# Four-layer graph network: layer norm statistics of the last groups, GpSimd waits for VectorE's port, a new written order

## The chip, the cores and the metric

The kernel runs on one core of a Trainium2 chip. The metric is the device time of one launch in microseconds; lower is better. All arithmetic is 32-bit floating point. Engines are named as in the profile: PE is TensorE (matrix products), DVE is VectorE, ACT is ScalarE, POOL is GpSimd and SP is SyncE, which here only issues DMAs.

## The reference

The input x has 128 graphs of 64 nodes with 256 features; adj is a 0/1 matrix of 64 x 64 for each graph. Four layers follow each other, each `x = layernorm(x + layer(x, adj))`:

```python
# layer 0: a GRU over the graph, five steps l
m = h @ weight[l];  agg = A.T @ m;  h = gru_cell(agg, h)      # A = (adj != 0); sigmoid and tanh gates
# layer 1: aggregation and a two-layer MLP (256 -> 1024 -> 256)
out = silu(rmsnorm((adj @ x + epsilon * x) @ W1 + b1)) @ W2 + b2
# layer 2: to the tangent space, aggregate, back to the ball
t = artanh(norm(x)) * x / norm(x);  s = adj @ t;  out = project(tanh(norm(s)) * s / norm(s))
# layer 3: attention with masked softmax
h = x @ W.T + b;  u = adj * exp(e[:, None] + f[None, :] + ab);  out = (u / sum(u)) @ h
```

What matters here is the layer norm at the end of each layer: mean and variance of each row of 256 features, then `(x - m) / sqrt(v + 1e-5)`.

## The kernel before

Two graphs are packed into a block of 128 rows; four blocks make a group, and there are 16 groups (g = 0 to 15, `NG` = 16). A group goes through all four layers in SBUF. The five GRU steps take by far the most TensorE time. Products by blocks (`gate`, `prod`, `by_sums`, `by_sums_back`) use seven products where plain block multiplication has eight, at the price of sums on VectorE.

The last group, 15, is cut into two pieces of two blocks after its MLP (layer 1), each a stream of its own, so that their short dependent steps overlap. They get `y1` and `adjT` from the group.

**Order.** `Flow` collects every instruction as an operation with an engine (or a choice of two), an assumed cost `us`, the buffers read and written, and for some the mark `port`. The string `ORDER`, made beforehand outside this file, says in which order the operations of up to six streams are issued, and on which engine. `issue` emits them and ties each to the one before it on its engine, so the order within an engine is fixed; between engines only data dependencies make waits. The assumed costs and the `kb` of DMAs have no other use in the file.

**Port.** Marked `port` are the GpSimd operations made by `pool` (sums `pool_sum`, powers, small ones `few` and `few_s`), and VectorE's elementwise work with all its operands in SBUF: `summing`, the updates of hT, `times_state`, `scaled` and `tan`.

**Statistics of a layer norm** (`layer_norm`). For groups 0 to 13 (`summed = g < NG - 2`):

- `onto_rows` (L811) writes y = product * scale + x and gives the sum of each row as a side output (`accum_out`) into `st`; for the second layer norm an extra ScalarE pass (L828) makes that sum.
- GpSimd makes the negative mean `mv`, ScalarE the sum of squared differences by a `Square` pass with side output (L833), GpSimd `ve`, the power `rstd` (L845) and the offset `off`.
- rows are scaled by ScalarE or VectorE.

For groups 14 and 15, VectorE makes the statistics with `bn_stats` (L841) and `bn_aggr` (L842) for each block, and `ve` (L843) and the offset (L854) as well; only the power stays on GpSimd. These two groups also run the small operations of layer 2 (norms, series, `onto_ball`) on VectorE, and the sums of squares `sqt` and `x3 + wb_r` by `summing` on VectorE, where the other groups use GpSimd's `pool_sum` (L448).

Other names below: `hr` (L790) is the DMA that turns hidden state into rows for the next aggregation, `x3T` likewise for attention; `ps_agg` is an aggregation, `p_ga` to `p_gc`, `p_hx`, `p_ix` GRU products, `ps_hr` (L782) the turn of the last hidden state into rows, `p_ah` to `p_ch` the first MLP product (L1109), `p_ox`, `p_oy` the second (L1184), `ps_o` the same for group 15 by plain products, `ps_sup` layer 2's aggregation, `ps_a`, `ps_att` attention; `w2f` sums (L681) prepare weights.

Of the kernel before, what the change touches and what calls it, by code (L numbers as in the profile page):

```python
# [53 lines left out]
class Flow:  # L54

    ENGINES, AHEAD = ("PE", "DVE", "ACT", "POOL", "SP"), 6
    SIGNS = "ABCDEFGHIJKLMNOPQRSTUVWXYZabcdefghijklmnopqrstuvwxyz0123456789!#$%&()*+,-./:;<=>"
    ORDER = ("CEEg~PhD~BNhED~BOiDC~Bs$CAAAAAAAAAAAAAAAAii~Nr~Nr~BO~N.~CU8~B+88~Bt~Bt8$~Bt~BL~Bt88li~BL~FU~FU~FU~FU"
             "~BL!i~Et~BL~Bt!~FZ~Bs~BL~FZ~BpEe~Bt~D%~BL~EO~BLA~DAi~DAB~DA~BoB~Bo~CUBF~BogiFFF~B+~B+HG~B+~GiAA~BK8~"
             "GjEC%~DB%B~BO%~FZAB~C3~BL~Es~E:~B<EA%B~CUlB~Et~BsB~CZBE~C5AB~CaE~BV~B+~C0~DiF,FA~D$H$~CBA~DE~CW~BsA~"  # L60
             "EQA$~BM~EQC&Ag~Dx~DBC~CV~DK~GK~Bs~CVgF&&~DxC~DGF%H~BsfBEF9(~EdA~B:AEj(jBB~Dx~D8~D8~MDAA~CJjkEBjFk~Mh"
             "x(~DA~Np~DAAx~MD~MDGl~BKT~NL~CJAH~DB~BdEA>CBAxe~Bdh~MBC~Lze~BpC~B+~Br!~BNxTA8TCG8~CB~CB~BN8B~J9!9DAD"
             "eAgDACCFB~CXCAAhBh~D8AKA~DABKK~DKKL~By~Do~BNLhFF~BV~BV#K~CAH#~G#PKhP~DA~Ce~B0~DA~Bt~DBKD~CAK~B0~BtPM"
             "~CAA~BV~By~IVA,P+CB8uh~BKA8A~Bp~Bq+gAC~BN~BNF;~BN~FZ~BNFBFBFuD~D%HFD~BQFKDGK~DjM~DF~Bu~BtL~Bt~Bt&M~B"
             "tMFHpFHFk%Fko&ooGoFqFGlopA(GpAlpH~BQA~BygG~CyoC&Ao&CoC~BQhAqGAG8Ag~BrBKGDKMA*DKgnKCh~DFnMDAPJBAKRDfK"
             "BD+B+B+~Bt~BQ~BQ~BQB+~JjEE~EP~D%E~BvpE~I3BK~BQB~BoA~DA~BqAA~BKA~B+~BoC~BM9~CUAA~BV~BVAAACBBC~Bo~Bo~B"
             "Veee!AC9FC~GAf~GAB8~CVABeGAg~EoC~Eo~BL~Bo(~BpA(AAAAB~CyAAKBKKAL!~BtA!kAA~BtCFCFBFFBFHFfHGKAAB~FeBKgK"
             "&CKkGKBMKKBKLBKK-~CA~CAKLM~ByM~ByMK~BU-KM~Bz~ByLK~BU~BVLKpKMKFBMFBKKBKMBKKBKK~BLEKE~BL~Ce~BL~Ce~Eo~C"
             "eEGEGLlL~DA~DA,,FKGKHKL~Bo~BoA~BqAAAG-~BoGC~BoK-9AG~BMAAGCAGAAB!88GC8ACBeeBgAfAC8B8B8BAGAGAC~Eo~BQJC"
             "*~EonA~BQ~BLAJA~BQAABAAAABAA~BMA!AfCACFF9FFBFHeBFfAFBFAgFBHFCKFBFBKqKGMFBHF~B:~B:H,~DALHo~B:L~B:~B:G"  # L70
             "F~BRp~CaKH~B;KFpH~BPBFBM~Bt~BtB%%LFBMBjlj~Bol~Buij~BLij~BL~BP~BLijEG%GL%jj~D8L~BQ~Cy~Bo&~DAFL~BR~H+L"
             "~BRF~H+L~BqF~BLHAALAA~B+~CBC~Bo~BqL~BMA~CUALAC~BVOA~BVAOB8ABsCeOB8CeGAgAfCB~GAF~GA8BA~CVAB~E+CA~BpjC"
             "kAA88AAABA~HUjBF~Bo!9A!AAlAHFGgeCGKKBKKKBMKfAGABFBg+G~CACK~BWBooBKBKM~Ce~BLoKB-~By~Byp~By~B0L~By~CeB"
             "q~CeMKB~HUMBKK~BziFE~BzFp~BUE~BL~BUE~EoL-oGop~Boq~CAp~CA~BL~CyGK~BLlK~BzM~Bo~BLFKG~DeHK~BLAAG~DAAG~B"
             "-A8CG~BoKG~BM8GAAG8CeAGfeBeeeeBg~BuACAgf8C8B~GAB~GAB8~B,AGAA~BQnC~Eo~BQJC~EoLAJ~BLAJ~BpAAABAAAABAA!A"
             "!FeCFFFCFHBF%BFfAABFBEgFGFCjBj(FB~B:~B:~B:BF~BtB(~Bt~Bt~BvGBjHAKHABAAoo~BpKBKLAAAAKG~BW~B:FBMB~BtBM~"
             "G%H~Bu~G%MFDG~BP~BMLF!~BQKgKGkHFCF~CaGFH~EtLDDHKLF~BQKDLCFK9gLFLCFqFDGFKFLFMFGAAFL~BRAACL(FALAALA8CL"
             "AeBA~D8BC8L8f~DAgpAA~CULCF~BVs~DKlAOBHA~BVsFG~BoOABAk~DKGABj~BV~By!kFg~ByFGDl~DKG~BV~DKAH~BVB~DK~DK~"
             "B0KGKK~B0KGC~By~CekM~ByC~CA,D+,~ByC~By~BU~B0B+~BWG~BV&KKMD~By~By~By~By~BWL8KqMAAGKGpCpAKCAAGK~BQAM*B"
             "LAJ~E:BK~BQKgAJ~BQJABCD~Bt~Bt~D%DC~CZ~IZDC~IZ~BQK~BQFFDFFK~CZH%~BvLFAAAAFBDFHFFGAA(AA~C3BH~BP~BPH~BP"  # L80
             "B~BPFlfKKB%~G%Gg+9j!B+KCBoHo~F*~FJ~E7~E7B!KK&gFLA!AA&ACAGKGCFApA-KGA~Bp-AjpqjBMAAlKBAF~Bu~EtLH~BtpA~"
             "Bt~BLoL~BtpFBKF~BL%LFfq~B:kKFL~BtfMA~D8~D8G~D8AAL(AAAL(AAApAFLAF,AAA9AAfFFL~ByfAHLAHAL~B+~B+~B+~B+~B"
             "Q~BY~B+A~BV~BysA~BKGs~CejkO~D+~BVA&AA~BVAAf~I8G~CefFB~BMF!~IeGGl~DKA~BVAH~FAK~BV~Ey~Ey~BQ~EyK~C!AGK~"
             "CeGK~CC~ByMkAAAG~BWAKG~JK~BU~CfK~CfKK,M~HyGo~BzoL-oKGqKMLnK~BQAnKMB~BdKLgK~BdKM~BQTK~BQCKT~BVKDLx!K>"
             "K!~CenCK~BzxCKLDKJDKD-T~BtK-~EPqKhhM~Bt~ErphoL~CZD~CZLh!~DFDpgDK~BQ~E:~BQFFgLKC~BaDFD~GjqDLF;DM~DjDD"
             "~B:D~FZHL~Bt~Bv~C3L~C3~BRF~Ca~E$~Bt~BP~E$~CaF~E$~CaCFDGDF~B:&DDCjGgjLgjAC~BQjLe~BRLeA~BML%g%Gg~CBjC~"
             "EPp~BRDFFL(FsDDFks~FA~BV~EyslF~BVHO~CZCG%~B:D&FDD&DF~BPGFDDF&(BF(~By9j~E$fH~ByBHKK~B0G~FAKKDG~EU~BM~"
             "Ce~BVFk!~D+~BVM~D++GC+C~CAl~C9F~C9KJ~BUGDK~C9HK~C9K~BWG~IeMDDKp~IALoLqoGM~BU~BUCGoCpogoGKqGGKMKCKKMB"
             "~Bt~BtoBKD~BVEKLEK~BuKEELFFFFFFKk~BWKKG-KGKMGKMIlp~E3(,P~C%LHoLp~C%PHKLPKII~CUqLPO~CUM~BoI~BRuAL~BKl"
             "eHL~CjpeHA!LFFCfIFFgfgeCe9CA~B,HABBBFRF999FF~BLBFHfjFB~E:H>~E:DgGKTKKFG!T%CGL%TFCFLl~D%D~BzH~D%D%~C5"  # L90
             "G%DFB!FkCKPGCKPPPlEGAAgF~CUBMD~CUFC~EUFGAAGCDGKCKIBMAA~BU+pC(H-AfADB~C8~C8KApoppAgDgDpKC~ByLH~DK~DK~"
             "CBCDKM~IACLK+L+DHMKL~GoKAAA,,A+pB+-ID~CfKLKM~By~ByLIAAAA~B,9IKKlBHH+HKK~CefFBFF9IBFHFFFF~CAFFH~BMBH!"
             "FGFG~D%G~D%%~BV%GCFF~Bqk~CZCL~CZ!%G%CBKFFkCKKGKf(~BtBl~BV~Bt~BuKFIMFMLoHAAMf9AAAAHALeHeeILA~BtHpK~BL"
             "MKGIAALLFFqfAAMAAf%HALAAALFFLAALeA~FALAA9AALA~DKfA~DKp~ByLeAAAf/A~DoG/~Bo~BoGs~Bo~BoFBO(AA~BVl888~BV"
             "AAIABFB~IeH~ByIHAAA~BzA~BMAIA~Bz!AABKHxK~EU~BVK~B7CKI~Do~Bd~DoLC~Do~By~B7~CgKD,T~BMK~C9K!>o~C9MTK~Cf"
             "FCTpFFLFoGKpMI~HyMCLoKpFF~CfhMFFkKDD&KlKKMDKD!KM~Ey#kklK~EyG~BUKKHDDhDK~C1DG~CBHKKkLHDDDDKDDHGKlKL!K"
             "GKGMKoM~DFpFqL~C3MLHFpFFKLKqL~Bt~Bt~BtG~Bt~BtM~Bt~BtFLFLFFLLL~By~By!~CeLp~DoDDDCDC~CeFL!8~B;C~DK/Asg"
             "sC~CZeOA~CZgCCkkkFFFCFF~BVF~BV~BVGkDFFFFFkFkF~B0F~CZ~CZDD~Ba~BV~CZ~DK~BV~DKGCF~DK~B0~BVD~DKDDDD~BV~D"
             "KKK;~B0KKM~By~By~By~ByKD9Bf~BWKMB~Ce~CeD~BMK,,oKL!KCKKCpKMDMKDMD~FAM~FA!LKKCBC+KK~C8BB~BOLKK,DKK$EL-"
             "EKKpKqKF~Bt,MLFoM~BP~BPL~BPpKKL~BPFFFLqk~BoMG~BoF~BRL88L(8L!~BM!L8LAAC~Fs~ByCFCLF~E$FFCFFCpFLAeOG/l~"  # L100
             "BVA~EyAOH~BVfO~C8BBIl~ByBYBl9~DPfYB~EZ~Ce~BEBl~DPBHfmBIDxC~BV~D:x~DKgI~IA~IA~BVKCKTK~BVKC~ByLIT~ByID"
             "~C8~Bil,D2KH,KYlDKILYgmKIY~BUm!LK~COKgLoLoCKI,IM~B$EKKDFDHGD~GjDkKKFML~DKk~DKD~CfKDKD;KKgFDM;DFDDk+g"
             "f+H,~C8~C8!~C8,~C8K~BVK~Cg,K~DKGMKL~BU--~BU~Bzo~BzK~BzM~BUp~BU~BuML~BUB~F8-poo~CBKp~ByM~ByB~ByKKKKKL"
             "~By~ByLKp~BWKK-KKq%,MFLoFLFpHKKLFLqFFMG~C3~BV8~BPL~BP~B:,8,F~BMA!LA,gFCL~BPjjLDlFH~BY~Bu~EyD&~DKC/D~"
             "DKGs~By~BV~ByOlGjH~DKGDDkDFDFGG~IADD~IAH~BV~BVK~BVKK~BVK~ByHM~ByG~BW~C8G+K~BW+kBKGKMpKLoooKG~BWKM~BV"
             "~BtM~G+KMLp+pGk~F8+KKqfM~EyGB~Bt*~CZKB*LD~BMKJ~BVJK~BQCKCKKKCKL~D%~BQ~Dj~BQDDL-DfKpKKK~BQ-~CZ~BQFMFF"
             "FKC~Bt~BtH9C~BQCFj,~B:MBj~BRFLEjHFiLo&i~BtDGEKpHjjLHjKGq~BtkFlL~BPH~G%G~GjMFG%G%LFlLF~BuH~EtL~Et~BV~"
             "BtA~BQ~Bt~Bu~BtLFLF%LFFkAG~B:CAC~BzF(~BzF~BzA(LFFOCAHs~BKHeOGCAOG9eCkACffFfCfACB~ByBFGAlJG~ByBBH~CeB"
             "f~CeB~DKG>K~B0KKTGK~ByMD~Do,~Dok~ByxCT~DKKkCok~BW~CeoCGKCK~BuMD~C8DK-L+~BW+Dq~ByLCF~BVFoMF~BVFMFFF,F"
             "KCG+Ck+CKG~E3EB~E:DG~BM~E:GCF~Et~B;KCk~C8CDKK~BuKH~Byp~EtDMF~BuDKKfCF~EPfFCDjFAGAAACFF~BVFA~BVAAGAF~"  # L110
             "BVCFAeAB(B(ACBFBAAAACAFClAAAHB8ABAGgAgAGkFCDAGC8FlD8GKC~BLK+CD~ByL~BoHBA~BWKGAGKC8GMAfAKB+KGg~CAKLgD"
             "~By~ByL-~ByA&MDA~BWKB~BUM~CeGMKg~Bz~HyC+~BzKLD~BUL~BU~BUGo-KGDKM*~EyM~ByLJ~EUJ~BzKLAJA~BVAA~BQ~BUKB~"
             "BQKDKKLK~Bt~BQLAAAA~EPB-~EPK~Bp~BvK-~EP~BQf~Bt~BvKBKKM9~D%MB~D%~Bv~CZL~CZ~DFLFFLFCFBKHK~BQCL%L%gF&FB"
             "qKHFLAGFM~BP~BPHLFHFLFH%G~GjH%gG~GFACG%G~F3CLFFBg~CUFHfAAHBFCA~BQA8AfAFLFF~BpAfAAAfAFfAAAGAAALAAeLFF"
             "pFeLeFGOAFOf~BRFfFs(~BVAAOAHkFHBAAA&AABAAGAAGeAAAA~BVBjF~BVkGAAAAlF~E7~FJB~E7~ByGA!AAHAAAA!GA~By~CnB"
             "KKGCTKK+CGx~CAMxD~BQ+g>~ByG+g>GKCxKGCKT~CAGMD~CAD~CAD~CA-LJ~CA~CCKJLq~C8~BtLJo~CBM~CB~CeJD~BUDD!K~Ba"
# [1326 lines left out]
```

## Time and profile before

| | us |
|---|---|
| median of 3 runs | 2286.3 (2285.16 to 2289.82) |
| the profiled execution | 2287.12 |
| its span, first to last instruction | 2284.7 |
| PE busy | 2239.7 |
| DVE busy | 1827.2 |
| ACT busy | 1304.0 |
| POOL busy | 533.6 |
| mean granted TensorE clock | 0.994 of full |

The span is what the profile shows; 2.4 us lie around it. Busy times are sums over the span. A time such as 2190 is in us from the span's start; a line such as L448 is a line of the kernel before, often that of a helper.

### The profile page before, as it was taken

To read this page: it belongs to the slowest core of one execution; us is meant where nothing else is said; L and a number is where in the kernel's file an instruction comes from. 1 tells how busy PE (TensorE), PEld (TensorE's weight loads), DVE (VectorE), ACT (ScalarE), POOL (GpSimd) and SP (SyncE) were. 2 spreads that over 40 slices of the span, in tenths; PEclk is the share of its full clock that TensorE was granted. 3 is DMA by queue.
4 is the path that set the end of the run, shared out by engine and by line. 5 is a ranking of instruction groups with operands and counts; after the bars stand their busy time and mean duration, and the time that the engine had idled before them with its cause. 6 is when DMAs were issued, how large, how long until landed. Compare 5 with 4: busy or idle time off the path is not lost.

```text
span 2284.7 us, 34183 instructions
## 1 busy us (share of the span) xinstructions
PE 2239.7 (98%) x12050; PEld 1983.1 (87%) x12050; DVE 1827.2 (80%) x3846; ACT 1304.0 (57%) x2842; POOL 533.6 (23%) x827
## 2 busy tenths in 40 slices
PE   8999999999999999999999999999999999999987
PEld 6888898888888898988989889898988989888875
DVE  6687788887887878888778887888788788877886
ACT  2444556665555656556565656656566565654565
POOL 4100213332213212132231212222122231210222
PEclk9999999999999999999999999999999999999998
DMA  5022112112212122121212212112221212211100
GB/s 155 15 29 37 22 28 59 19 22 47 56 15 45 37 31 56 22 40 28 35 40 36 51 22 39 39 29 47 31 37 29 40 38 35 42 29 19 33 20 28
DMA packets 430042, 84.58 MB, mean 37 GB/s; under 512 B 399236, under 2 KB 428960, under 8 KB 429872
## 3 DMA queue, kind: packets, MB, share of 16 engines
q1 hardware_dynamic: 428144, 80.52, 19.8%
q8 instruction: 95, 1.56, 0.3%
q10 hardware_dynamic: 1328, 1.31, 0.2%
q0 software_dynamic: 400, 0.57, 0.1%
q14 instruction: 75, 0.61, 0.1%
HBM read 32.55 MB, written 8.39 MB: 18 GB/s over the span
## 4 chain that ended last, share of the span: by engine, by line
PE 92%; DVE 4%; DMA 2%; SPq 1%; ACT 1%; issue 1%; POOL 0%; POOLq 0%; DVEq 0%; ACTq 0%
PE p_ga L926 23%; PE p_gc L926 11%; PE ps_agg L399 7%; PE p_ix L932 6%; PE p_hx L932 6%; PE p_gb L926 6%; PE p_ah L1109 5%; PE p_iy L932 4%; PE p_ox L1184 4%; PE p_hy L932 4%; PE p_oy L1184 3%; PE p_ch L1109 2%; PE ps_a L399 2%; PE ps_wmih L399 1%; PE ps_sup L399 1%; DMA hr<-t 1%
## 5 line engine op out<-in xcount | busy, mean ns | idle before, releaser
L442 POOL TENSOR_SCALAR mv<-st 128x4 f32<-128x4 f32 x56 | 16.3, 292 | 767.5 <-ACT x_n L828 422.6
L926 PE MATMUL p_ga<-hT,w_h 128*128 128x256 f32 x640 | 177.7, 380 | 1.1 <-DVE hT L1051 1.0
L926 PE MATMUL p_gc<-tA,w_h 128*128 128x256 f32 x640 | 178.5, 380 | 0.1
L926 PE MATMUL p_ga<-tA,w_h 128*128 128x256 f32 x640 | 177.7, 381 | 0.0
L926 PE MATMUL p_gc<-tB,w_a 128*128 128x256 f32 x640 | 175.7, 380 | 0.7 <-DVE tB L445 0.7
L926 PE MATMUL p_ga<-agg,w_a 128*128 128x256 f32 x640 | 173.3, 380 | 0.3 <-DVE agg L426 0.3
L926 PE MATMUL p_ga<-tB,w_a 128*128 128x256 f32 x640 | 171.8, 379 | 0.0
L399 PEld LDWEIGHTS ps_agg<-edge,hr 128*128 128x128 f32 x1024 | 148.3, 191 | 17.4 <-issue 2.8
L399 PE MATMUL ps_agg<-edge,hr 128*128 128x128 f32 x1024 | 152.4, 276 | 3.2 <-DMA hr<-t 3.2
L979 ACT ACTIVATE U<-U,half_b 128x512 f32<-128x512 f32 (+1 forms) x160 | 95.1, 629 | 91.2 <-DVE U L976 91.2
L430 ACT ACTIVATE hnb<-p_hx,half_b 128x256 f32<-128x256 f32 x197 | 92.6, 471 | 92.0 <-PE p_hx L932 74.5
L926 PEld LDWEIGHTS p_ga<-tB,w_a 128*128 128x128 f32 x640 | 120.3, 190 | 16.4 <-DVE tB L445 0.3
L926 PEld LDWEIGHTS p_gc<-tB,w_a 128*128 128x128 f32 x640 | 119.7, 190 | 17.0 <-DVE tB L445 1.3
L926 PEld LDWEIGHTS p_gc<-tA,w_h 128*128 128x128 f32 x640 | 118.7, 190 | 16.0 <-DVE U L992 0.5
L926 PEld LDWEIGHTS p_ga<-agg,w_a 128*128 128x128 f32 x640 | 118.2, 190 | 16.1 <-DVE agg L426 1.2
L926 PEld LDWEIGHTS p_ga<-hT,w_h 128*128 128x128 f32 x640 | 117.2, 190 | 16.1 <-DVE hT L1051 1.2
L926 PEld LDWEIGHTS p_ga<-tA,w_h 128*128 128x128 f32 x640 | 116.8, 191 | 15.8 <-ACT U L425 1.5
L979 ACT ACTIVATE V<-V,half_b 128x256 f32<-128x256 f32 (+1 forms) x160 | 89.1, 587 | 69.2 <-DVE V L976 68.7
L845 POOL TENSOR_TENSOR rstd<-ve,pow 128x4 f32<-128x4 f32 (+2 forms) x67 | 79.8, 1191 | 137.0 <-DVE ve L843 128.3
L992 DVE TENSOR_TENSOR V<-p_ix,V 128x256 f32<-128x256 f32 x192 | 80.6, 421 | 34.6 <-PE p_ix L932 30.3
L425 ACT COPY agg<-ps_agg 128x512 f32<-128x512 f32 x131 | 76.2, 583 | 47.2 <-PE ps_agg L399 45.8
L1184 PE MATMUL p_oy<-w2f,hid 128*128 128x128 f32 x720 | 101.1, 278 | 0.5 <-ACT hid L1160 0.4
(289 smaller groups left out, 6152.5 us busy)
## 6 DMA issues: line engine op xcount, KB each, us to landing
hr<-t SPq DMA_DIRECT2D x256, 128.0 KB, 3.8
x<-in_x_dram SPq DMA_DIRECT2D x64, 128.0 KB, 2.6
xr<-in_x_dram SPq DMA_DIRECT2D x16, 512.0 KB, 3.4
xs<-in_x_dram SPq DMA_DIRECT2D x120, 64.0 KB, 2.4
out_dram<-x_n SPq DMA_DIRECT2D x15, 512.0 KB, 2.9
x3T<-t SPq DMA_DIRECT2D x56, 128.0 KB, 3.8
edge<-in_adj_dram SPq DMA_DIRECT2D x64, 32.0 KB, 2.3
wm<-in_L_gnn_weight_dram SPq DMA_DIRECT2D x5, 256.0 KB, 3.8
```

Of the source, the lines that this page charges most:

```text
L399: return nc.tensor.matmul(o, lhsT, rhs, start=(k == 0), stop=(k == nk - 1))
L425: flow.either([("ACT", on_act(n, r), lambda: nc.scalar.copy(o(), i())), ("DVE", 0.145 + 0.00105 * n, lambda: nc.vector.tensor_copy(o(), i( ...
L430: flow.either([("ACT", on_act(n, r) if in_bank(r) else on_act(n + 108, r), lambda: nc.scalar.activation(o(), i(), AF.Identity, bias=bias() ...
L442: pool(0.23, lambda: nc.gpsimd.tensor_scalar(w[0](), x(), s0, s1, op0, *((op1,) if op1 else ())), [w[1]], r)
L845: pool(0.41 + 0.625 * m, lambda: nc.gpsimd.tensor_tensor(rstd[:, :m, :], ve[:, :m, :], pow2[:, :m, :NB], OP.pow), [rstd], [ve])
L926: pe(HR, lambda i=i, w=w, c=c: nc.tensor.matmul(ps[:, c * HR:(c + 1) * HR], w[:, m, c * P:(c + 1) * P], v[i][0](), start=first and i == 1 ...
L932: pe(HR, lambda: nc.tensor.matmul(ps[:, j * HR:(j + 1) * HR], w[:, m, :], v[0](), start=first, stop=True, skip_group_check=True), [ps], [( ...
L979: act(HR if len(w) == 1 else R, lambda: nc.scalar.activation(o(), src(), AF.Tanh, bias=half_b[:, i * KD + c:i * KD + c + 1], scale=0.5), w ...
L992: dve(HR + 6, lambda: nc.vector.tensor_add(uu[:, c, half(n)], region(ps, j), uu[:, c, half(n)]), [(uu, (n, c))], [ps, (uu, (n, c))])
L1109: pe(HR, lambda c=c: nc.tensor.matmul(ps[:, c * HR:(c + 1) * HR], w1f[:, w, (2 * q + c) * P:(2 * q + c + 1) * P], v[0](), start=first and ...
L1184: pe(128, lambda j=j, k=k: nc.tensor.matmul(ps[:, i * HR + j * P:i * HR + (j + 1) * P], val(v[k // 2])[:, k % 2, j * P:(j + 1) * P], w2f[: ...
```

## The change

- Groups 14 and 15 get their row sums by side output too, and their squares by ScalarE. Group 14 becomes a `summed` group altogether: its small operations, its `sqt` sums and its mean and offset go to GpSimd. For group 15, VectorE makes `mv`, `ve` and offset from the sums; `x3 + wb_r` goes to GpSimd in all groups. The pieces of group 15 take over the group's `st1`.
- A GpSimd operation marked `port` whose assumed cost is over 0.4 us waits, by a semaphore, for the last `port` operation of VectorE that is ahead of it in the order.
- Some assumed costs differ, and `ORDER` is another string (left out below).

```diff
+    LONG = 0.4
-    ORDER = ("CEEg~PhD~BNhED~BOiDC...
+    ORDER = ("CE#AAAEgDAAAhDECAAAD$...
+    AFTER = mybir.DependencyInfo(mybir.DependencyClass.Sync, mybir.DependencyReason.DATA)
...
-        last = {}
+        last, held = {}, None
         for eng, o in self.placed():
             made = o.ways[eng][1]()
+            if eng == "POOL" and eng in o.port and o.us > self.LONG and held is not None:
+                self.tc.add_manual_dep(made.ins, held.ins.name, self.AFTER, reason="the port in the plan's order")
...
                 last[eng] = i
+            if eng == "DVE" and eng in o.port:
+                held = last[eng]
...
-        flow.op("PE", {512: 0.863, 256: 0.433, 128: 0.219, 1: 0.2}.get(n, 0.3), run, w, r)
+        flow.op("PE", {512: 0.86, 256: 0.432, 128: 0.223, 1: 0.223}.get(n, 0.3), run, w, r)
...
-                    [(xs, (c, q))], kb=16 * n)
+                    [(xs, (c, q))], kb=36 * n)
...
-                edge[s][m::Q, :n, quads[t]], ..., [(edge[s], m)], kb=8 * n)
+                edge[s][m::Q, :n, quads[t]], ..., [(edge[s], m)], kb=14 * n)
...
-                flow.op("SP", 0.6, ..., [(dst, ("q", q))], [t], kb=32 * NB)
+                flow.op("SP", 0.7, ..., [(dst, ("q", q))], [t], kb=70 * NB)
...
-        summed = g < NG - 2
+        summed = g < NG - 1
...
-                    **(dict(accum_out=st[:, b, 0:1]) if summed else {}))
-            dve(340 if summed else 256, run, [(y, b), *([(st, (0, b))] if summed else [])], [ps, (x, b), *r])
+                    accum_out=st[:, b, 0:1])
+            dve(340, run, [(y, b), (st, (0, b))], [ps, (x, b), *r])
...
-            if summed and of:
+            if of:
                 for b in range(NB):
-                    act(364, lambda b=b: nc.scalar.activation(
-                        o[:, b, :], y[:, b, :], AF.Identity, accum_out=st[:, b, 0:1]), [(o, b), (st, (0, b))], row(b))
+                    act(256, lambda b=b: nc.scalar.activation(
+                        o[:, b, :], y[:, at + b, :], AF.Identity, accum_out=st[:, at + b, 0:1]), [(o, b), (st, (0, at + b))], row(b))
             if summed:
-                few_s((lambda: mv[:, :, 0], mv), lambda: st[:, :, 0], -1.0 / D, OP.mult, [st])
...
+                few_s((lambda: mv[:, :, 0], mv), lambda: st[:, at:at + NB, 0], -1.0 / D, OP.mult, part(0))
+            else:
+                dve(4, lambda: nc.vector.tensor_scalar(mv[:, :, 0], st[:, at:at + NB, 0], -1.0 / D, None, OP.mult), [mv], part(0))
+            for b in range(NB):
+                act(364, lambda b=b: nc.scalar.activation(
+                    o[:, b, :], y[:, at + b, :], AF.Square, bias=mv[:, b, 0:1], accum_out=st[:, at + b, 1:2]),
+                    [(o, b), (st, (1, at + b))], [*row(b), mv])
...
             else:
-                for b in range(NB):
-                    dve(256, lambda b=b: nc.vector.bn_stats(st[:, b, :], y[:, at + b, :]), [(st, b)], row(b))
-                    dve(4, lambda b=b: nc.vector.bn_aggr(mv[:, b, :], st[:, b, :]), [(mv, b)], [(st, b)])
-                dve(8, lambda: nc.vector.tensor_tensor(
-                    ve[:, :m, :], over(mv[:, :, 1], m), eps2[:, :m, :NB], OP.add), [ve], [mv])
+                dve(8, lambda: nc.vector.scalar_tensor_tensor(
+                    ve[:, :m, :], over(st[:, at:at + NB, 1], m), 1.0 / D, eps2[:, :m, :NB], OP.mult, OP.add), [ve], part(1))
...
-                return y1, adjT
+                return y1, adjT, st1
...
-            y1, adjT = piece[3:]
-            st1 = stats()
+            y1, adjT, st1 = piece[3:]
...
-        (pool_sum if summed else summing)(NB * D, lambda: x3.tile(), lambda: x3.tile(), lambda: over(wb_r.tile(), NB), OP.add, [x3], [x3, wb_r])
+        pool_sum(NB * D, lambda: x3.tile(), lambda: x3.tile(), lambda: over(wb_r.tile(), NB), OP.add, [x3], [x3, wb_r])
```

## The prediction

> **What bounds the kernel now.** I read the page's first two parts, then TensorE's waits, then the timeline around the longest of them.
>
> The page, parts 1 and 2 (busy time and share; busy tenths in 40 slices of 57 us):
>
> ```profile
> PE 2239.7 (98%) x12050; PEld 1983.1 (87%) x12050; DVE 1827.2 (80%) x3846; ACT 1304.0 (57%) x2842; POOL 533.6 (23%) x827
> PE   8999999999999999999999999999999999999987
> ```
>
> TensorE is the bound, and the change leaves its 6212 compiled matrix instructions as they are. So time can only come from its idle time, 2284.7 - 2239.7 = 45 us: nothing in the profile allows more. By stretches: 7 us in the first 40, 11 between 60 and 2150, some 27 after 2150, where the last two groups (14 and 15) have no later group behind them to fill the gaps.
>
> TensorE's waits (line, releaser, us in total, times, longest):
>
> ```profile
> PE ps_hr L782 <- DVE hT L1051: 3.5, 3, 1.9
> PE ps_agg L399 <- DMA hr<-t: 3.2, 5, 0.9
> PE ps_o L399 <- ACT hid L1160: 2.3, 1, 2.3
> PE p_hx L932 <- DVE tA L445: 2.2, 1, 2.2
> PE p_ch L1109 <- DVE ts L445: 2.0, 2, 1.6
> PE ps_a L399 <- DMA x3T<-t: 1.6, 2, 0.9
> ```
>
> Most of them name VectorE. The timeline says why it was late (first VectorE, then GpSimd, around 2190; then VectorE at 2207):
>
> ```profile
> 2189.91 0.65 DVE L1049 SCALAR_TENSOR_TENSOR hT<-U,hT 128x512 f32<-128x512 f32 x1
> 2190.60 2.72 DVE L1051 SCALAR_TENSOR_TENSOR hT<-hT,V 128x512 f32<-128x512 f32 x1
> ...
> 2190.14 2.63 POOL L448 TENSOR_TENSOR x_n<-x_n,wb_r 128x1024 f32<-128x1024 f32 x1 [4.47 <-DVE t L1366]
> ...
> 2207.55 2.30 DVE L854 SCALAR_TENSOR_TENSOR few<-mv,rstd 128x4 f32<-128x4 f32 x1 [1.03 <-POOL rstd L845]
> ```
>
> L1051 usually takes 0.69 us; here it takes 2.72 and ends just when GpSimd's sum does. The 2.30 us of L854, a 0.15 us instruction, are the same with GpSimd's xb sum (2207.48 to 2209.82). I went through all VectorE instructions in the trace: 41 are over 0.25 us longer than the median of their kind, each with a long GpSimd instruction beside it; the excess is 41 us. TensorE gaps that follow such a one within some us: 2.25 and 1.16 before 34 us (four w2f sums at 24.8 to 30.5 hold up tA and its queue); 0.34, 0.45, 0.64, 0.38, 0.50, 0.22, 0.83, 0.88 and 0.72 in the middle, 5.0 together; 1.95, 0.21 and 1.64 after 2190. Sum 3.4 + 5.0 + 3.8 = **12.2 us**. Gaps that end with a DMA landing (hr or x3T): 0.95, 0.86, 0.77, 0.65, 0.88, 0.47, **4.6 us**.
>
> **What the Trainium skill says.** "SBUF — State Buffer", section Who interferes with whom: a VectorE instruction with two SBUF inputs and a GpSimd one that reads SBUF exclude each other; the first to start holds the port for its whole length. The trace agrees (2.72 us for 0.69). "GPSIMD Engine Reference", section 3.1: a two-input elementwise instruction takes 1.96 times as long on GpSimd. Here the 128x512 sqt sum is 1.31 us there and 0.69 on VectorE, 1.9 times. "TensorE: Matmul & The Clock Gate", section What's actually happening: TensorE's clock is halved after an idle window. The stretches table agrees in direction; the third number from the end is the granted clock:
>
> ```profile
> 2220.00:2240.00 20.00, 13.40 (x68) 11.43 (x67) 13.31 (x32) 15.62 (x35) 3.42 (x5) 0.74 0.01 2
> ```
>
> **The change, part by part.**
>
> *Port waits.* A GpSimd instruction with a planned cost over 0.4 us (sums, powers) now waits for the last port-holding VectorE instruction ahead of it in the plan. In the compiled orders, long GpSimd instructions with a VectorE wait go from about 64 to about 200 of some 310. The wait doesn't free the port: a sum that the plan puts first still holds VectorE up, but then the plan knew it. It stops sums from running ahead, the case at 2190. Behind a waiting GpSimd instruction stand only GpSimd's own; it is busy 23%, and those who wait for it are the layer norms (rstd, off, x_n) and the rms power. Gain: 0 to 12.2 us. I take three quarters, 9, since one and the same wait should remove most, and the head (3.4) has a new order with the same five w2f sums. Cost: up to one 0.69 us VectorE instruction on each of 64 layer norms' powers; in the middle groups the other five streams cover that (11 us idle in 2090), so nothing taken, bound +15 (a third of the 64 reaching TensorE).
>
> *Costs and kb.* Nothing in the file reads kb, and costs only enter the 0.4 test; they act through the order. The DMA figures rise from 16 to 36, 8 to 14 and 32 to 70 per block, and hr from 0.6 to 0.7, so an order made with them leaves more room before an aggregation. Bounds 0 and 4.6; taken 3.
>
> *Statistics of groups 14 and 15.* VectorE loses 32 bn_stats (24 x 0.42 + 8 x 0.41 = 13.3 us) and 32 bn_aggr (4.9); it gains 28 accumulator reads at 0.084 (2.4) and 7 small mv at 0.16 (1.1): -14.7. Group 14's sums leave too: seven sqt (7 x 0.69 = 4.8), x_n plus wb_r (1.2 + 2 x 0.68 = 2.6) and some 25 small ones at 0.17 (4): about -26 in all. ScalarE gains 32 squares and 4 identities, 0.50 us each in a row with the accumulator read (36 x 0.5 = 18 us); GpSimd 49 instructions: 7 x 1.31 + 2.44 + 2 x 1.2 + 15 for three short powers, two long and small ones at 0.27, about 29. ScalarE is busy 66 of the 100 us from 2150 and GpSimd 24, so both have the time; the point is latency. Per half-group layer norm of 15, two bn_stats and two aggregates (1.2 us) become one mv (0.2), two squares (1.0) and two engine changes (0.1 to 0.3 each): +0.3 alone. There are three in a row behind ps_o, +1; against it, VectorE is dense from 2263 to 2279 and loses there about eight rows x 0.6 = 4.9 us, of which I count 2. Group 14's chain gets longer by four identities (2.0), by powers in place of reciprocals and small ones at 0.27 for 0.17 (some 6): +8, behind group 15's 128 ps_o (17.1 us) and what follows them (34 us).
>
> *Order anew.* In the compiled order of TensorE group 14's p_ox and p_oy (112 x 0.11 = 12.3 us) now stand among group 15's p_ah, p_bh, p_ch. There the gaps from 2219 to 2233 are 0.35 + 0.68 + 0.78 + 1.52 + 1.37 + 2.25 = 6.9 us; I count 5 filled. But they had covered the way from hr over the layer norm to the ea aggregation (2194 to 2205): y, mv, four squares (2.0), power 1.0, x_n make about 6.7 us with only four att and four rms left to run: -5. And ps_sup of group 14 now stands inside ps_o, after 34 of 128: from its last xb the chain is identities 2.0 + squares 2.1 + GpSimd 6.5 + Ln with table 1.5 + 1.1 + tan 0.5 and hops, some 15 us; TensorE is there after about 13: -2. Sum of the tail: +5 - 5 - 2 - 1 + 2 = **-1** (loss), with bounds of 6 either way, since the tail's new waits are not in this trace. SyncE's 617 issues are the same in another order; the DMA engines are busy about a fifth of the time, so only when an hr or x3T is issued counts, and that is in the 3 above. The middle's new order has the same instructions; taken 0 beyond the above.
>
> **Sum:** 9 + 3 - 1 = 11 us off the profiled execution, 2284.7 of span and 2287.1 in all: 2276.1. The median of the runs, 2286.3, is 0.8 lower; I keep **2276**.
>
> **Rivals.**
> B, *the gaps move*: half the port and DMA gaps return elsewhere (6 gained) and the tail loses 5: 2286. For it: the 27 us of tail are latency, not work, and every filler was already in use. Against: 12 us of gaps have one cause that the change names.
> C, *GpSimd's waits become TensorE's*: a power queued behind VectorE, which is 80% busy and in order, delays x_n, the aggregation and then everything in TensorE's fixed order. At 0.69 us for a third of the 64 norms 15 us, less 6 gained: 2296. It decides from some 15 norms on (10.6 / 0.69), or from 10 us of new waiting in the tail. For it: at 2190 VectorE was itself 2 us late, and GpSimd would now inherit that. Against: GpSimd is idle three quarters of the time, and before 2150 no wait of TensorE on it is listed.
> D, *the waits are not there*: excluded by the compiled order, except where an older wait covers them.
>
> **Numbers.** A (as forecast) 0.66, own range 2268 to 2281.7; B 0.16; C 0.18. 0.2% is 4.6 us, about what a measurement of this kernel can tell from no change: faster is below 2281.7, slower above 2290.9. The low end of the range is 12.2 + 4.6 + 4 = 20.8 off, 2266; the high end takes in B and the near part of C, 2292.
>
> **What would show it.** Right: no L1051 or L445 much over 1 us, VectorE's excess below 15 us, TensorE's idle between 60 and 2150 at 6 us or less, hr and x3T gone from its waits, p_ah and p_ch without gaps in the tail. Wrong: new waits of TensorE on GpSimd's rstd or on x_n, ps_sup waiting over 4 us, or the last 35 us grown by over 3.

## The result, and the profile after

The changed kernel takes 2273.07 us (median of 4 runs, 2270.57 to 2274.23) where the kernel before took 2287.02 on the same chip (2285.16 to 2289.82): a ratio of 0.9937, interval 0.9919 to 0.9954, some 14 us less. The forecast was 2276 and 11 us less. The profiled execution took 2273.74 us, its span is 2271.9 (before: 2287.12 and 2284.7), and the mean granted clock is 0.994 in both.

The page after, the same two lines as were shown of before (busy time and share; busy tenths in 40 slices):

```profile
PE 2232.8 (98%) x12050; PEld 1983.3 (87%) x12050; DVE 1782.1 (78%) x3778; ACT 1324.0 (58%) x2910; POOL 541.6 (24%) x876
PE   8999999999999999999999999999999999999986
```

TensorE's idle time fell from 45.0 to 39.1 us, but its busy time fell too, by 6.9 us, with the same 12050 records. The loss was thus never only in the idle time. Two things hide it. First, records overlap: a 128x256 matmul has a record of 0.38 us, while the next one starts after 0.216 us, so a stall of up to 0.16 us shows no idle time at all, and a longer one shows 0.16 too little. Second, the granted clock: in some stretches of these traces it stands at 0.5 of full, and the matmuls there take longer without any idle time.

To count all of it, I take the time from the start of one matmul to the start of the next, less the median for its line and shape. So counted, TensorE lost 60.2 us before and 44.1 after, between its first and its last matmul. Of the 45.0 us of idle time 11.4 lie outside these two, so the parts are:

| us lost between the first and the last matmul | before | after |
|---|---|---|
| idle | 33.6 | 28.3 |
| in matmuls that start at half clock, idle time apart | 8.3 | 6.1 |
| hidden in the other records | 18.4 | 9.6 |

TensorE's waits after (us in total, times, longest):

```profile
PE ps_warm L1261 <- DVE few L1288: 5.5, 1, 5.5
PE ps_agg L409 <- DVE x_n L441: 4.9, 1, 4.9
PE ps_o L409 <- ACT hid L1173: 4.2, 1, 4.2
PE ps_agg L409 <- DMA hr<-t: 3.5, 2, 3.0
...
PE ps_sup L409 <- ACT tan L1317: 1.0, 2, 0.7
```

(`ps_warm` are transposes whose result nothing reads.) The waits for hT, for tA and for x3T are gone from the top, so the middle is nearly free of stalls by VectorE. The three longest waits all lie after 2150, and a wait of 3.0 us for one hr stands alone at 469.7. VectorE's instructions held up by over 0.25 us beside a long GpSimd instruction went from 41 with 41.0 us of excess to 19 with 14.7.

### The profile page after: what moved, and what is told of

It is laid out like the page before. It is cut to its first block, busy times and chain, and to the rows that moved or that the text cites. A ratio compares the mean times of both kernels' runs of the same rounds, so it can differ in the third digit from the quotient of the medians.

```text
span 2271.9 us, 34322 instructions
## 1 busy us (share of the span) xinstructions
PE 2232.8 (98%) x12050; PEld 1983.3 (87%) x12050; DVE 1782.1 (78%) x3778; ACT 1324.0 (58%) x2910; POOL 541.6 (24%) x876
## 4 chain that ended last, share of the span: by engine, by line
PE 94%; DVE 2%; DMA 1%; ACT 1%; SPq 0%; issue 0%; POOL 0%; POOLq 0%; DVEq 0%; ACTq 0%
PE p_ga L939 24%; PE p_gc L939 12%; PE ps_agg L409 8%; PE p_ix L945 6%; PE p_hx L945 6%; PE p_gb L939 6%; PE p_ah L1122 5%; PE p_ox L1197 5%; PE p_iy L945 5%; PE p_hy L945 4%; PE p_oy L1197 4%; PE p_ch L1122 2%; PE ps_a L409 2%; PE ps_sup L409 1%; PE p_bh L1122 1%; PE ps_att L409 1%
## 5 line engine op out<-in xcount | busy, mean ns | idle before, releaser
L939 PEld LDWEIGHTS p_ga<-tA,w_h 128*128 128x128 f32 x640 | 116.8, 190 | 17.3 <-ACT U L435 2.0
L848 ACT ACTIVATE x_n<-y,mv 128x256 f32<-128x256 f32 x192 | 95.3, 499 | 33.5 <-POOL mv L452 29.2
L458 POOL TENSOR_TENSOR sqt<-sqt,sqh 128x512 f32<-128x512 f32 x60 | 76.6, 1277 | 145.6 <-DVE tA L455 47.5
```

Of the source, the lines that this page charges most:

```text
L458: pool(0.24 + 0.00203 * n, lambda: nc.gpsimd.tensor_tensor(o(), x0(), x1(), op), w, r)
L848: act(364, lambda b=b: nc.scalar.activation(o[:, b, :], y[:, at + b, :], AF.Square, bias=mv[:, b, 0:1], accum_out=st[:, at + b, 1:2]), [(o ...
L939: pe(HR, lambda i=i, w=w, c=c: nc.tensor.matmul(ps[:, c * HR:(c + 1) * HR], w[:, m, c * P:(c + 1) * P], v[i][0](), start=first and i == 1 ...
```

## The experiments

The change has separable parts: the **waits** (a few lines in `issue`), the **plan** (the order up to a point near 2000 us, where the old and the new order have issued the same operations but four), and the **end** (statistics and the order of the last two groups). The plan is not the order alone: the string also picks the engine where there are two, and the new plan puts 17 instructions on ScalarE that the old one has on VectorE (3829 on VectorE in e3, 3846 in e2). All ratios below are to the kernel before on the same chip, each with its 95% interval; the times are medians, and differences taken from them can be up to 1 us apart from what the ratios say. "Excess" is the time by which VectorE's instructions beside a long GpSimd one exceed the median of their kind.

| kernel | waits | plan | end | us | ratio | excess, us |
|---|---|---|---|---|---|---|
| before | no | old | old | 2285.2 to 2287.0 | 1 | 41.0 |
| e1 | no | new | new | 2293.5 | 1.0035 (1.0023, 1.0048) | 52.2 |
| e2 | yes | old | old | 2270.9 | 0.9934 (0.9921, 0.9946) | 12.4 |
| e3 | yes | new | old | 2272.4 | 0.9944 (0.9932, 0.9957) | 12.4 |
| e4 | yes | old | new | 2268.7 | 0.9925 (0.9913, 0.9938) | 15.4 |
| e5 | sums only | old | old | 2270.8 | 0.9933 (0.9920, 0.9947) | 11.8 |
| e6 | 30 long sums | old | old | 2276.6 | 0.9955 (0.9943, 0.9968) | 25.1 |
| e7 (after) | yes | new | new | 2272.8 | 0.9940 (0.9928, 0.9953) | 14.7 |
| e8 | yes | old | new, 8 moved | 2269.9 | 0.9926 (0.9913, 0.9938) | 14.8 |
| e9 | yes | old | new statistics, old order | 2293.1 | 1.0025 (1.0016, 1.0034) | 13.1 |
| e10 | on any VectorE | old | new | 2277.8 | 0.9958 (0.9945, 0.9970) | 27.8 |
| e11 | on any VectorE | old | new, sum late | 2277.6 | 0.9956 (0.9942, 0.9969) | 28.6 |
| e12 (= e4) | yes | old | new | 2270.2 | 0.9924 (0.9912, 0.9937) | 14.8 |

**The changed kernel without the waits.** The orders on all five engines are those of after.

```diff
-    LONG = 0.4
+    LONG = 99.0
```

> The kernel after with LONG raised from 0.4 to 99, so that no GpSimd instruction waits for the port; order and instructions on every engine are the same. Theory W (the waits carry the gain: they stop sums from running ahead into VectorE): VectorE's excess in instructions beside a long GpSimd one goes back from 14.7 us to 35 or more, and the time rises by 6 to 10 us, to 2279 to 2283, a ratio to the kernel before of 0.997 to 0.998. Theory O (the order carries it, and the waits would be worth nothing without or with it): within 2 us of the kernel after, 0.993 to 0.9945. Theory C (the waits cost TensorE time of their own): faster than the kernel after, below 0.993.

It is 8 us slower than the kernel before, and some 22 us slower than after (ratios 1.0035 and 0.9940). The loss against after is twice what the theory of the waits expected, and the new order with the new statistics, without the waits, is worth less than nothing. One place shows it. First VectorE and GpSimd without the waits, then TensorE:

```profile
1437.99 2.19 DVE L1064 SCALAR_TENSOR_TENSOR hT<-hT,V 128x512 f32<-128x512 f32 x1
...
1437.27 2.36 POOL L458 TENSOR_TENSOR x_n<-x_n,wb_r 128x1024 f32<-128x1024 f32 x1 [7.88 <-DVE t L1378]
...
1440.33 0.63 PE L792 MATMUL ps_hr<-ident,hT 128*128 128x128 f32 x4 [1.05 <-DVE hT L1064]
```

The sum ran as soon as its data were there, 0.7 us ahead of hT; hT ended only at 1440.2, half a microsecond after the sum, and TensorE waited 1.05 us for hT. The same place in the kernel after:

```profile
1426.15 0.69 DVE L1064 SCALAR_TENSOR_TENSOR hT<-hT,V 128x512 f32<-128x512 f32 x1
...
1427.34 2.36 POOL L458 TENSOR_TENSOR x_n<-x_n,wb_r 128x1024 f32<-128x1024 f32 x1 [9.78 <-ACT U L435]
```

There the sum comes behind hT. (The profile puts its wait down to U on ScalarE, which ended 0.02 us behind VectorE's tB; the sum waited for both engines.) Over the whole trace, of the sums that start after more than 0.1 us of idle time, the profile puts 14 of 91 down to VectorE in e1 and 54 of 94 in after. In this place the sum holds up ea instead (1.94 us for 0.75, at 1428.32), and TensorE does not stop for over 0.16 us.

**The kernel before with the waits alone.**

```diff
+            if eng == "POOL" and eng in o.port and o.us > self.LONG and held is not None:
+                self.tc.add_manual_dep(made.ins, held.ins.name, self.AFTER, reason="the port in the plan's order")
...
+            if eng == "DVE" and eng in o.port:
+                held = last[eng]
```

> The kernel before with the port waits added and nothing else: its own order, its own statistics. Theory W: the excess falls from 41 us to about 15, and with it about three quarters of the 12.2 us of TensorE gaps behind blocked VectorE instructions: 9 us less, 2278, ratio 0.996. Theory O: the waits alone change nothing or lose, since the old order was not made for them: 0.999 to 1.002. Theory C: GpSimd's powers and sums come late and TensorE waits on x_n and rstd: above 1.003.

14 us faster by the medians, 15 by the ratio: the whole gain of the change, with the order and the statistics of before. Excess fell as expected, from 41.0 to 12.4; the gain is some 60% larger than the 9 us of the forecast. Its page:

```profile
PE 2232.4 (98%) x12050; PEld 1980.4 (87%) x12050; DVE 1800.0 (79%) x3846; ACT 1303.9 (58%) x2842; POOL 523.1 (23%) x827
```

With a span of 2267.6 us, TensorE is idle 35.2 us, 9.8 less than before, though the span is 17.1 shorter; from start to start its loss fell by 17.3 (60.2 to 42.9). Of this, 10.0 are idle time, 4.4 are matmuls at half clock (8.3 to 3.9) and 3.0 are hidden in the other records. The half clock has a place. In the kernel before it comes right behind two of the stalls that the prediction lists, from 26.8 and from 2194.2 us on, for 3.4 us each. In e2, and in e5 below, there is none in the head and none there. Two stretches of before and two of e2 (the third number from the end is the granted clock):

```profile
20.00:40.00 20.00, 16.59 (x59) 11.04 (x58) 17.52 (x29) 5.66 (x17) 7.55 (x7) 0.91 0.76 210
2180.00:2200.00 20.00, 15.98 (x112) 14.60 (x111) 17.76 (x37) 9.33 (x20) 6.46 (x6) 0.91 0.27 53
...
0.00:60.00 60.00, 53.62 (x253) 39.88 (x254) 33.69 (x89) 17.82 (x45) 26.60 (x44) 1.00 0.56 148
2150.00:2180.00 30.00, 28.14 (x176) 24.90 (x174) 27.27 (x56) 25.40 (x54) 9.01 (x19) 1.00 0.07 19
```

The size of this part is rough: two profiles of one kernel, e4 and e12 below, differ in it by 2.7 us.

**The two halves of the order.** The operations are those of before for the first and of after for the second; only the string `ORDER` is joined from the two at the point named.

```diff
-    ORDER = (the old plan, the old end)
+    ORDER = (the new plan to operation 12040, then the old end's rest)
```

> The kernel before (old statistics of groups 14 and 15) with the port waits, the new order up to the point near 2000 us where both orders have issued the same instructions but four, and the old order from there. Theory W with a neutral end, as forecast (head and middle +12, tail -1 with the statistics): 11 to 12 us below the kernel before less what the waits save in the old tail, so equal to the kernel after within 3 us, 0.9935 to 0.996. Theory T (the gain is in the last two groups: statistics and their order): at most 5 us below the kernel before, 0.998 or more.

```diff
-    ORDER = (the new plan, the new end)
+    ORDER = (the old plan to operation 12040, then the new end's rest)
```

> The kernel after (waits, new statistics) with the old order up to the same point near 2000 us and the new order from there: the other half. Theory W with a neutral end: it gains only what the waits take out of the old head and middle, some 5 us, and the tail gives about 0: 0.997 to 0.999. Theory T: nearly the whole gain, 0.995 or less. The gains of this and of the new plan with the old end need not add up to 14 us, since the old head and middle have the waits here.

All four pairings of plan and end, with the waits, lie within 0.2% of each other (e2, e3, e4, after). The new end is 1 to 2 us better than the old one (0.9925 against 0.9934, 0.9937 and 0.9940 against 0.9944), which single intervals don't separate. The new plan is 2 to 3 us worse. The stages say the same: from the matmul that stands at 60 us in after to the one at 2000, by count, after takes 1940.1 and e7 1940.9 us, e4 and e12 1936.1 and 1935.7, e2 1934.8 and e3 1938.1. The expectation of e4 rested on the waits giving only 5 us in the old plan; they gave three times that.

**Which waits.** Sums alone, and the long sums alone, in the kernel before:

```diff
-            if eng == "POOL" and eng in o.port and o.us > self.LONG and held is not None:
+            if eng == "POOL" and eng in o.port and o.us > self.LONG and round(o.us, 3) not in (1.035, 1.04, 1.66) and held is not None:
```

> The kernel before with the port waits on GpSimd's sums alone; its 142 powers (planned at 1.035, 1.04 and 1.66 us) wait for nothing. In the traces so far every VectorE instruction that was held up stood beside a sum, none beside a power. Theory S (only sums hold the port): the excess stays near 12 us and the time is that of all waits, 0.9934 of the kernel before, within 0.001; if the powers' waits cost layer norms some time, up to 0.001 faster. Theory P (powers hold it too, or their waits set the pace in some other way): the excess goes to 25 or more and the ratio to 0.996 or more.

```diff
-    LONG = 0.4
+    LONG = 2.0
```

> The kernel before with the port waits on its 30 sums of 128x1024 alone (planned at 2.319 us; LONG at 2.0). They stand beside 17 of the 41 us of excess. So far the time followed the excess at about half a microsecond for each (28.6 us less gave 14.3 us in the kernel before, 37 more cost 20 in the new order). Theory D (dose): excess 24 to 26, 7 to 9 us faster, 0.9962 to 0.997. Theory B (only the long sums hurt TensorE, the 1.3 us ones are absorbed): nearly the whole 14 us, 0.994 or less. Theory N (waits act through all of GpSimd's order, and a tenth of them does little): 0.9985 or more.

Without the 142 powers' waits the time is the same (0.9933 against 0.9934): they bring nothing and cost nothing. With the 30 long sums alone 16 of the 41 us of excess go and 10 us of time: theory D, with a little more time than its 7 to 9 us. Across these kernels the time follows the excess at 0.5 to 0.65 us for each: 15 for 28.6 (e2), 10.3 for 15.9 (e6), 22 for 37.5 (e1 against after).

**After once more, and its end reordered.**

> The kernel after unchanged, for its time on the same chip as the next one and for a second profile. 0.9925 to 0.995 of the kernel before. A second profile should show again the 3.0 us wait for hr near 469 us if the new order issues those loads too late (theory L), and not if that was chance.

The wait for hr is there again, at the same place, as it was in e1 and e3 (3.2 and 3.0): it belongs to the new plan. First SyncE's queue, then TensorE, in e7:

```profile
465.83 3.42 SPq L800 DMA_DIRECT2D hr<-t  x4
...
472.40 1.13 PE L409 MATMUL ps_agg<-edge,hr 128*128 128x128 f32 x8 [3.08 <-DMA hr<-t]
```

The four issues take 3.4 us, the last starts at 468.6, and landing takes 3.9 in the median, while TensorE is there at 469.3. In the old plan the largest wait for an hr is 1.1 us. In after, e1 and e7 the clock then stands at half for 3.4 us, from 473.7, 474.0 and 473.8 us on; in e3, with the same wait, it does not. The same stretch in after and in e3:

```profile
473.70:477.10 3.40, 3.40 (x14) 3.05 (x13) 2.88 (x7) 2.26 (x5) 2.92 (x8) 0.51 0.42 66
...
473.70:477.10 3.40, 3.40 (x18) 3.00 (x17) 2.83 (x7) 3.40 (x8) 2.67 (x9) 1.00 0.12 18
```

TensorE loses another 1.5 us there in after and 1.6 in e7. The wait and the half clock together are most of what the new plan costs between 60 and 2000 us: 4.5 of 5.3 us in after, 4.7 of 6.1 in e7, and 3.0 of 3.3 in e3, each against e2. That earlier issues would win this time back is not shown: no run moves them.

```diff
-    ORDER = (e4)
+    ORDER = (e4, eight operations of VectorE and GpSimd moved after 2170 us)
```

> The kernel with the old plan and the new end, with eight operations of VectorE and GpSimd moved in the last 90 us: piece a's small chain (L1282, L1285, L1287) ahead of group 14's y, GpSimd's rstd of piece b ahead of group 14's squares, GpSimd's 128x1024 sum of group 14 a few operations away from L1334, which it had held up for 0.8 us, denominators of group 13 behind more urgent work. TensorE's work is the same. Theory Q (TensorE's waits of 4.9, 4.2 and 5.5 us in the end are queue places on VectorE, ScalarE and GpSimd): 2 to 4 us below the old plan with the new end, 0.991 to 0.9917. Theory R (they are the length of the chains, whatever the places): no change, 0.992 to 0.9935.

No change (0.9926 against e4's 0.9925), and TensorE's three long waits are the same to 0.02 us. The expectation of 2 to 4 us missed: L1282 did move ahead of two y, but L1283 still came behind all of them, and the long sum still held L1334 for 1.80 us. So these moves settle nothing on whether places or chain lengths make those waits; that stays open.

**The statistics without the new order.**

```diff
-    ORDER = (the new plan, the new end)
+    ORDER = (the old order throughout; each new operation where its last input is written, those that need it behind it)
```

> The code of the kernel after (waits, statistics by side outputs, group 14's small operations on GpSimd) in the old order from the first operation to the last: TensorE's and SyncE's orders are the old ones, each new operation stands where its last input is written. Against the kernel before with the waits alone (0.9934 in its run) this is the statistics by themselves. Forecast of the prediction: three norms in a row behind ps_o lose 1 us, VectorE's relief gives 2, group 14's longer chain is hidden: 0.993 to 0.9945. Theory L (latency decides: squares, powers and small GpSimd operations lengthen every norm of the last two groups): 3 us or more slower than the waits alone, 0.995 or more. Theory V (VectorE's 26 us less load is what the end needed): 3 us or more faster, 0.992 or less.

21 us slower than the waits alone: theory L, far beyond its size. Up to 2146 us the two are even; from there to the end this one takes 142.6 us and e2 121.3. Its waits, by TensorE, and one of them in ScalarE's timeline:

```profile
PE ps_T L778 <- ACT x_n L436: 5.3, 2, 3.0
PE ps_att L405 <- ACT hw L1390: 4.8, 3, 2.8
```

```profile
2197.17 0.51 ACT L844 ACTIVATE x_n<-xb,mv 128x256 f32<-128x256 f32 x1 [0.46 <-POOL mv L448]
...
2199.43 0.47 ACT L1390 ACTIVATE hw<-ps_a,hw 128x256 f32<-128x256 f32 x1
...
2199.95 0.70 PE L405 MATMUL ps_att<-hw,adjT 128*128 128x257 f32 x2 [2.78 <-ACT hw L1390]
```

Four squares of a layer norm (L844, with their accumulator reads 2.1 us) and the two passes ahead of them stand before hw in ScalarE's queue, and TensorE waits 2.78 us for hw. ScalarE is busy 96.6 of the last 143 us, so over the whole end it has time; it is the place in its queue that makes this wait. Where the new operations stand was my choice; another placing in the old order could cost less. What it shows is that these statistics lose 21 us in this placing, while in the new order of the end the same statistics come with a net gain of 1 to 2 us: the places decide.

**More waiting.** The waits of e4, but on VectorE's last instruction of any kind, and on sums alone; then with one sum later besides:

```diff
-            if eng == "DVE" and eng in o.port:
+            if eng == "DVE":
```

> The old plan with the new end, where a GpSimd sum waits for the last VectorE instruction of any kind ahead of it in the plan (not only the two-input sums), and powers wait for nothing. 15.4 us of excess are left in that kernel, about half of it on instructions that the waits don't know (hT L1059, V L991, ea L1076, few L1334). Theory D (the time follows the excess at one half): excess to about 8, 3 to 4 us faster than the old plan with the new end, 0.9905 to 0.9915. Theory E (what is left lies beside work that TensorE does not wait for, or sums come so late that layer norms wait): the same time or up to 3 us slower, 0.9925 to 0.994.

> As the one before, and GpSimd's last sum of 128x1024 (group 14's x_n plus wb_r) is put behind the small chains of both pieces (L1334 to L1346), one of which it had held up for 0.8 to 1.6 us. Theory Q (these chains carry the end): a further 0.8 to 1.6 us, seen in the gap before ps_att of 0.84. Theory R: no change, since group 14's own chain becomes the last.

> The old plan with the new end unchanged, for its time on the same chip as the three others: 0.992 to 0.9935 of the kernel before, and the same TensorE waits of 4.9, 4.2 and 5.5 us.

The excess does not fall to 8, it rises to 27.8, and the time rises by some 8 us (0.9958 against e12's 0.9924): the expectation missed in sign, while time and excess still go together. One place, in e12 (VectorE, then GpSimd):

```profile
1439.30 1.14 DVE L450 TENSOR_TENSOR hT<-hT,V 128x512 f32<-128x512 f32 x1 [0.65 <-ACT V L1051]
...
1437.52 2.37 POOL L453 TENSOR_TENSOR xb<-x_n,b_r 128x1024 f32<-128x1024 f32 x1 [1.70 <-DVE few L1404]
```

and in e10:

```profile
1444.23 2.39 DVE L450 TENSOR_TENSOR hT<-hT,V 128x512 f32<-128x512 f32 x1 [0.64 <-ACT V L1051]
...
1443.72 2.35 POOL L453 TENSOR_TENSOR xb<-x_n,b_r 128x1024 f32<-128x1024 f32 x1 [3.40 <-DVE y L816]
```

In e12 the sum waits for the last instruction with its operands in SBUF (few L1404) and then runs beside y and V, which read PSUM and take their usual 0.48 and 0.42 us; hT loses 0.45. In e10 it also waits for y, starts half a microsecond before hT and holds hT for 1.7 us. The same is seen over whole kernels. Of the time of the 128x512 and 128x1024 sums on GpSimd, w2f's apart, about 45% lay beside VectorE instructions with an operand in PSUM and 31% beside others in the kernel before; 56% and 14% in e2; 38% and 37% in e1; 46% and 22% in e10. And the first kind is not held up: in the kernel before 175 VectorE instructions with an operand in PSUM started inside a sum, and none took over 0.01 us more than its median. Of 61 others 38 took over 0.25 us more. So the waits of the change help by putting sums beside VectorE's PSUM work, not by making them late. The late sum of e11 changed nothing that can be seen.

## Why the prediction was right, step by step

- **TensorE's idle time as the whole pool** (45 us, "nothing in the profile allows more"): wrong as a premise. Part of the loss hides inside busy time, in overlapping records and at half clock; from start to start it was 60.2 us. And 11.4 of the 45 lie ahead of the first matmul and behind the last, where no gap between matmuls can be closed.
- **Port waits, +9:** the mechanism is right and the size was too small; alone they give 14 to 15 us. The term was three quarters of 12.2 us of listed gaps, and the gaps understate the stalls that they stand for, by what is hidden in the records and by the half clock (together 7.4 of the 17.3 us that e2 wins from start to start). Counting the excess (28.6 us removed) at one half, a rate that only the runs gave, comes to 14. One reading is off: at 2190 L1051 does not end "just when GpSimd's sum does" (2192.77) but 0.55 us later, as hT does in e1.
- **Powers that wait, cost 0:** right by e5. The bound of +15 was far off, since nothing of it was seen.
- **DMA gaps, +3 from the order:** wrong in sign. x3T's wait went, but hr's went from 3.2 to 3.5 us with one of 3.0 that the old plan does not have, and the half clock behind it took 1.5 more; the new plan costs 2 to 3 us.
- **Statistics, worked out by instruction counts:** the net of end and statistics, forecast at -1, is a gain of 1 to 2 us, within the bounds of 6. The loads came near the counts (e9 against e2: VectorE 20.7 us less for 26, ScalarE 17.1 more for 18, GpSimd 24.9 more for 29). But the parts were not small: as e9 places them, the statistics in the old order lose 21 us. That ScalarE and GpSimd "have the time" was read from busy shares; the place in a fixed queue decides.
- **Order of the end:** hr to the ea aggregation was forecast to open a gap of 5 us: 4.89 measured. p_ah to p_ch stand without gaps, as forecast. ps_sup inside ps_o was to wait 2 us: no wait, and it stands behind 68 of the 128 records of ps_o, where 34 were counted. Not foreseen: ps_o's start now waits 4.2 us (before 1.4 and 2.3 in a row), and from ps_o's end to the last instruction it is 36.8 us in place of 34.3, where a gain of 1 (2 less 1) was counted.
- **The marks:** VectorE's excess is 14.7 (under 15 forecast); TensorE's idle between 60 and 2150 is 7.5 (6 forecast, missed by that hr); ps_sup's waits are 1.0 in all, in the middle groups; the last part grew by 2.5, under 3. Two marks failed: "no L1051 or L445 much over 1 us", but in after these two lines (L1064 and L455 there) still reach 1.46 and 2.29 us. And TensorE has a new wait on x_n, named as a sign of being wrong: it is the 4.89 us just told, which the tail's sum had counted as a gap.
- **Rivals:** B (gaps move) and C (waits become TensorE's) did not come. C's mechanism, a GpSimd instruction that waits for too much, is seen in e10, but through VectorE: the sum comes late and then blocks. The argument against C that no wait of TensorE on GpSimd is listed before 2150 overlooks the start, where ps_x waits 2.6 us for ident; it does so after the change too.

So the total was near in part by luck, through errors that cancel: waits 15 where 9 was counted, plan -3 where +3 was counted, end +2 where -1 was counted. Their sum, 14, is what the runs show. The first is clear of the noise; the other two are near the width of the intervals.

The old plan with the waits and the new end is the fastest that was run (e8 is the same within 0.0002): 0.9925 and 0.9924 in two runs, against 0.9937 and 0.9940 for the change. The intervals overlap, so the 3 us between them lean on the stage times as well (4 to 5 us less between 60 and 2000).

## What to carry to other kernels

Where GpSimd and VectorE both work on operands in SBUF, ask of each long GpSimd sum what VectorE does beside it, and tie the sum to the point after which VectorE reads PSUM; a wait on too much took back 8 us of some 17. Price a stall from start to start of the matmuls, not by idle time, and look at the granted clock behind it. Price a moved operation by its place in its new engine's queue, not by that engine's share of busy time. Judge an order and the waits apart, in all pairings: the new order, with its statistics, was 8 us worse than the old one without waits, and still no better with them, so the gain of the whole change was the waits' gain.

## What the runs showed of the hardware

A power on GpSimd did not hold VectorE up, though one on 128x4 lasts 1.04 us. In the kernel before 31 VectorE instructions of 128x512 with two SBUF operands started inside one of the 142 powers; their mean excess is 0.001 us, the largest 0.03. 27 such started inside a sum; their mean excess is 0.57, the largest 2.15. The Trainium skill, "SBUF — State Buffer", section Who interferes with whom, states the exclusion for a GpSimd instruction that reads SBUF; the sums agree with it here, and the powers, on 128x2 to 128x8, do not show it.
